# A two-layer graph network on one core: the planner of the instruction order gets a new table of TensorE's switches and tile durations, and new aims

## The chip, the cores and the metric

The kernel runs on one core of one Trainium2 chip, as one program. The time is the device time of one execution in microseconds (us). Five engines work side by side, each through a list of instructions of its own, in order: TensorE (PE in the profile; its weight loads are told apart as PEld), VectorE (DVE), ScalarE (ACT), GpSimd (POOL) and SyncE (SP, which only issues DMAs here). They wait for one another by semaphores.

## What is computed

Sixteen graphs (B = 16) of 1024 nodes with 256 features each, and an adjacency matrix of whole numbers for each. Two layers follow one another:

```python
# layer 0: attention of 8 heads of 32, masked by the graph, one linear map, residual
q, k, v = heads(x @ Wq), heads(x @ Wk), heads(x @ Wv)
e = einsum('whqd,whkd->whqk', q, k)
e = where(e >= 0, e, 0.2 * e)
attn = softmax(where(adj > 0, e, NEG), axis=-1)
h = layernorm(attn @ v)
x = layernorm(concat([h, x]) @ Wffn.T) + x
# layer 1: two graph attentions, layer norm, feed-forward of width 1024, layer norm
for W, a in ((W1, a1), (W2, a2)):
    Wh = h @ W                                  # h starts as x
    e = leaky_relu(Wh @ a[:256] + (Wh @ a[256:]).T, 0.2)
    h = softmax(where(adj > 0, e, NEG), axis=1) @ Wh
h = layernorm(x + h)
out = layernorm(h + relu(h @ w_ff1 + b_ff1) @ w_ff2 + b_ff2)
```

All of it is float32.

## The kernel before

For each batch (graph) `b` there are two kinds of work. The **attention of layer 0** is 8 heads of 8 tiles of 128 keys, 64 tiles for a batch. For each tile TensorE makes the scores of 128 keys by 1024 queries (line 612, two matmuls of 512 columns; the planner calls this kind `single`), ScalarE and VectorE make the leaky relu of them (lines 628 and 630), ScalarE the exponential (line 633), GpSimd multiplies by the mask of the graph (line 637), and the result `p` goes to the product with the values `v` (line 652). That product has only 32 output rows, so four matmuls, each for a quarter of the queries, lie side by side in TensorE's columns; the planner calls this kind `narrow`. The sums of the weights come from the same kind of product with a column block of minus ones. Two of these products a head are saved by adding tiles on VectorE first (line 682, `add_pair`): tiles 0 and 1, and tiles 2 and 3. So a head has 8 narrow products with `v` and 6 with minus ones. They are issued in groups of two tiles, four groups a head, 512 groups in all.

The **wide work** is all else on TensorE, the planner's kind `None`: projections of the next batch (lines 489 and 521), transposes (lines 369, 436, 702 and 846), the linear map of layer 0 (lines 778 and 781), both graph attentions (lines 901 and 926) and the feed-forward (lines 966 and 994). All of a batch after its attention is started by `rest(b)`, and runs while the attention of batch b+1 runs. The projections and the mask of batch b+1 are started by `project(b + 1, t0)` when the attention of batch b begins. Batch 0's attention therefore has nearly no wide work beside it, and the rest of batch 15 has no attention beside it.

The order in which every engine gets its instructions is planned in Python when the kernel is built. Each piece of work is a generator that yields its next operation with a cost in ns (`on(PE=880)`), waits for events, takes and gives buffers, and has an **aim**, the time at which it is due. `Order.run` keeps a clock for each engine, looks for the operations that could start within 300 ns of the earliest, takes the one with the smallest aim, emits its instructions, and moves the clock on by the cost. For TensorE it adds to the cost an entry of `SWITCH`, found by the kind of the operation before and the kind of this one; a pair that is not in the table costs nothing. A wrong cost changes no result and no instruction; it makes the plan believe that something is ready earlier or later than it is.

The aims come from two tables of shares of `SLOT` (253 us): `EARLY` for what belongs to the first batches, `AIM` for the others. `share(b, name)` chooses: `EARLY` for b below 2. For `project(b)` the choice is by b-1, so the projections and masks of batches 1 and 2 go by `EARLY`. `mask` and `mask_step` give the due times of the eight parts of the next mask after the start of the batch, `x` those of the input, `qk0`, `qk1`, `v0` and `v1` those of the projections; `rows`, `first0`, `graph0`, `second`, `normed` and so on those of the steps of `rest(b)`, and `ff` those of the feed-forward of its four pairs of row tiles. `pace(b)` says how fast the scores of a batch fall due; `fast0`, `fast1` and `fast15` stretch it for batches 0, 1 and 15. `lead` says how long before its due time a score tile may start.

Buffers that matter for the order: 6 tiles `p`, 2 score tiles in PSUM, 3 `misc` tiles in PSUM, 18 `pair` buffers, 2 masks, and one `job` for the feed-forward, so that there is one feed-forward at a time.

Of the kernel before, what the change touches and what calls it, by code (L numbers as in the profile page):

```python
# [34 lines left out]
class Order:  # L35
# [5 lines left out]
    HOP = dict(PE=53.0, ACT=35.0, DVE=36.0, POOL=80.0, SP=60.0)  # L41
    TAIL = dict(PE=163.0, ACT=103.0, DVE=84.0, POOL=42.0, SP=0.0)
    WINDOW = 300.0
    SWITCH = {(None, "narrow"): 93.0, ("single", "narrow"): 93.0, ("narrow", None): 93.0,
              ("narrow", "single"): 197.0, (None, "single"): 84.0}

    STRETCH = 3413.0
    WORK = 0.43
# [89 lines left out]
    def run(self):  # L138
        while self.active:
            could = []  # L140
            for th in self.active:
                costs, shared, delay, mode = th["op"]
                best = None
                for engine, cost in costs.items():
                    ready = th["ready"] + self.HOP[engine]
                    if th.get("last", ())[:2] == (engine, th["ready"]):
                        ready -= self.HOP[engine] + self.TAIL[engine]
                    t = asked = max(self.clock[engine], ready)
                    if shared and engine in ("DVE", "POOL"):
                        t = max(t, self.port[engine])  # L150
                    if best is None or t + cost < best[0] + best[2]:
                        best = t, engine, cost, asked
                could.append((best, th))
            first = min(c[0][0] for c in could)
            (t, engine, cost, asked), th = min((c for c in could if c[0][0] <= first + self.WINDOW),
                                        key=lambda c: (c[1]["aim"], c[1]["no"]))
            if th["op"][1] and engine in ("DVE", "POOL"):

                before = [c for c in could if c[1]["op"][1] and c[0][1] in ("DVE", "POOL")
                          and c[0][1] != engine and c[0][3] < asked]  # L160
                if before:
                    (t, engine, cost, asked), th = min(before, key=lambda c: (c[1]["aim"], c[1]["no"]))
            costs, shared, delay, mode = th["op"]
            self.active.remove(th)
            if engine == "PE":
                cost += self.SWITCH.get((self.mode, mode), 0.0)
                self.mode = mode
            end = self.clock[engine] = self.end(engine, t, cost)
            self.busy[engine] += cost
            if shared and engine in ("DVE", "POOL"):  # L170
                if engine == "DVE":
                    self.port["POOL"] = end - 54.0
                else:
                    self.port["DVE"] = end - 130.0
            self.now = t
            th["ready"] = end + self.TAIL[engine]
            th["last"] = engine, th["ready"]
            if delay:
                self.transfers = max(self.transfers, end + 1000) + 1450 * max(1, round(cost / 500))
                th["ready"] = max(end + delay, self.transfers + 1200)  # L180
                th["last"] = None, 0
            self.step(th, engine)
        stuck = {k: len(v) for k, v in list(self.waiting.items()) + list(self.queues.items()) if v}
        assert not stuck, f"threads that never end: {stuck}"


def on(shared=False, delay=0.0, mode=None, **costs):
    return "on", (costs, shared, delay, mode)
# [6 lines left out]
def wait(event):  # L195
    return "wait", event
# [37 lines left out]
def unshifted_path(  # L234
# [8 lines left out]
    nc = tc.nc  # L243
# [9 lines left out]
    G = 4  # L253
    GV = 2
    QN = N // 4
    ADDED = 2
    YW = D + 2
    NSUM = NT * H + 2 * NT
    NSCORE = 4 * NT
# [1 line left out]
    PACE = SLOT / (H * NT // 2)  # L261


    AIM = dict(mask0=0.7454, x=0.7836, x_step=0.0012, mask=0.7416, mask_step=0.0241, qk0=0.8169, qk1=0.7629,
               qk_step=0.0234, v0=0.8897, v1=0.9566, v_step=0.0513, rows=-0.1328, rows_step=0.039, first0=0.1101,
               first1=0.2264, graph0=-0.041, graph1=0.3629, graph_step=0.0128, second=0.3518, second_step=0.0609,
               normed=0.8572, normed_step=0.058, ff_wait=(None, 0, 1, 0), ff=(0.6792, -0.0021, 0.5781, 0.4984),
               ff_step=0.0549, fast0=0.4291, fast1=0.9756, fast15=0.6646, lead=1.5024)

    EARLY = dict(x=0.9697, x_step=0.0004, mask=0.7306, mask_step=0.0331, qk0=0.7893, qk1=0.9441, qk_step=0.026,  # L270
                 v0=0.8496, v1=0.9733, v_step=0.0532, rows=-0.1833, rows_step=-0.0236, first0=0.1365,
                 first1=-0.0311, graph0=-0.0903, graph1=-0.027, graph_step=0, second=0.3474, second_step=0.0327,
                 normed=0.781, normed_step=0.02, ff_wait=(None, 0, 1, 0), ff=(0.6698, 0.0209, 0.488, 0.4266),
                 ff_step=0.0422)

    const = ctx.enter_context(tc.tile_pool(name="const", bufs=1))
    sb = ctx.enter_context(tc.tile_pool(name="sb", bufs=1))
# [123 lines left out]
    def mask_part(b, t, halves):  # L401
# [29 lines left out]
        yield take("misc")  # L431
        pt = misc(BF)
        pairs = ab.bitcast(BF)
        yield on(PE=112 * n)
        for i in range(2 * n):
            nc.tensor.transpose(pt[:, i * P:(i + 1) * P], pairs[:, i * P:(i + 1) * P], ident_b)
        yield give("adjb")
# [20 lines left out]
    def x_pair(b, u):  # L458
        yield take("pair")
        xr = buf([P, 2, D], "pair", "xr")  # L460
        yield pause(1500)
        yield on(ACT=400, delay=3500)
        nc.scalar.dma_start(xr, x[b, u * 2 * P:(u + 1) * 2 * P, :].rearrange("(p i) d -> p i d", p=P))
        yield take("misc")
        pt = misc()
        yield on(PE=437)
        transposes(pt, [xr[:, i, :] for i in range(2)])
        yield give("pair")
        engine = yield evacuate(2 * D)
# [44 lines left out]
    def v_part(b, g, u):  # L514
        yield wait(("xT", b, u))
        yield take("misc")
        pa = misc()
        yield on(PE=880)
        for i in range(2):
            for dc in range(DC):  # L520
                nc.tensor.matmul(pa[:, i * P:(i + 1) * P], xTs[b][:, dc, (2 * u + i) * P:(2 * u + i + 1) * P],  # L521
# [69 lines left out]
    def all_scores():  # L591
        for b in range(B):
# [4 lines left out]
            for h in range(H):  # L597
                yield wait(("stack", b, h))
                q, kk = stacks[b, h]
                for t in range(NT):  # L600
# [5 lines left out]
                    else:  # L606
                        yield aim(t0, BIG)
                    ps = psum.tile([P, N], FT, tag="scores", name="ps_s")
                    yield on(PE=464, mode="single")
                    for nh in range(NH):  # L610
                        cols = slice(nh * HALF, (nh + 1) * HALF)
                        nc.tensor.matmul(ps[:, cols], kk[:, t * P:(t + 1) * P], q[:, cols], start=True, stop=True)  # L612
# [27 lines left out]
    def all_values():  # L640
        for b in range(B):
            for h in range(H):
# [9 lines left out]
                        nc.tensor.matmul(acc[i * DH:(i + 1) * DH, at:at + QN], w, p[:, i * QN:(i + 1) * QN],  # L652
                                         start=first, stop=last)

                added = []
                for d in range(0, NT, GV):
                    last, adds = d + GV == NT, d < ADDED * GV
                    for t in range(d, d + GV):
                        yield wait(("p", b, h, t))
                    if added:  # L660
                        yield wait(("p added", b, h, d - GV))
                    yield aim(begin[b] + (h * NT + d + 2) / 2 * pace(b), SLOT)
                    ps = [probs.pop((b, h, t)) for t in range(d, d + GV)]
                    for t, p in zip(range(d, d + GV), ps):
                        yield on(PE=430, mode="narrow")
                        product(v[:, t, c:c + DH], p, 0, t == 0, False)
                        yield aim(begin[b], BIG)
                    if adds:
                        yield start(add_pair(b, h, d, ps), begin[b] + (h * NT + d + 2) / 2 * pace(b))
                    for p in added if adds else added + ps:  # L670
                        yield on(PE=430, mode="narrow")
                        product(minus_ones, p, QN, False, last and p is ps[-1])
                        yield give("p")
                    added = ps[:1] if adds else []
                yield start(after_head(b, h, acc), begin[b] + (h + 1) * NT // 2 * pace(b))
                if h % G == G - 1:
                    yield give("v")
            yield start(rest(b), work.now)

    def add_pair(b, h, d, ps):  # L680
        yield on(DVE=1180, shared=True)
        nc.vector.tensor_tensor(ps[0], ps[0], ps[1], op=OP.add)  # L682
        yield give("p")
        yield fire(("p added", b, h, d))

    def after_head(b, h, acc):
        if h == 0:
# [9 lines left out]
        yield give("acc")  # L697
        yield take("misc")
        pt = misc()
        yield on(PE=437)  # L700
# [50 lines left out]
    def rows_pair(b, u):  # L751
# [12 lines left out]
        yield on(PE=437)  # L764
        transposes(pt, rows)
        yield fire(("hn used", b, u))
        yield take("pair")
# [20 lines left out]
        yield take("pair")  # L788
        yield take("misc")
        pt = misc()  # L790
        yield on(PE=437)
        transposes(pt, rows)
        yield give("pair")
        yield wait(("b2", b, u))
# [9 lines left out]
        for t in tiles:  # L804
            yield take("misc")
            pa = misc()
            yield on(PE=880)
# [28 lines left out]
    def first_half(b, s, nh):  # L836
# [4 lines left out]
            yield wait(("row", b, s, t))  # L841
        yield take("misc")
        pt = misc()
        yield on(PE=437)
# [70 lines left out]
    def normed_pair(b, u, big, y2):  # L915
# [6 lines left out]
        for i, t in enumerate(tiles):  # L922
            for half in range(2):
                yield on(PE=1728)
                for j in range(half * NT // 2, (half + 1) * NT // 2):
                    nc.tensor.matmul(pa[:, i * D:(i + 1) * D], big[:, j, t * P:(t + 1) * P], y2[:, j, :D],  # L926
                                     start=(j == 0), stop=False)
            yield on(PE=218)
            as_rows(pa, i, x1, i)
        yield fire(("weighed", b, u))  # L930
        yield give("pair")
# [4 lines left out]
        rT = buf([P, DC, 2 * P], "pair", "rT")  # L936
        yield take("misc")
        pt = misc()
        yield on(PE=437)
        transposes(pt, rows)  # L940
        yield give("pair")
        for dc in range(DC):
# [37 lines left out]
    def feed_forward(b, u, rT):  # L980
# [9 lines left out]
        for i in range(2):  # L990
            for half in range(2):
                yield on(PE=1728)
                for hc in range(half * HC // 2, (half + 1) * HC // 2):
                    nc.tensor.matmul(pa[:, i * D:(i + 1) * D], hid[hc // 2][:, hc % 2, i * P:(i + 1) * P], wf2[:, hc, :],  # L994
                                     start=(hc == 0), stop=False)
            yield on(PE=218)
            as_rows(pa, i, rT, i)
        for _ in range(HC // 2 + 1):
            yield give("pair")
# [471 lines left out]
```

## Time and profile before

| what | value |
|---|---|
| median of 3 runs | 4397.64 us (4397.36 to 4398.8) |
| the profiled execution's own time | 4397.53 us |
| span of its instructions | 4395.7 us |
| mean granted clock of TensorE | 0.99 |
| TensorE busy | 4246.0 us, 97% of the span |
| VectorE, ScalarE, GpSimd busy | 81%, 68%, 55% |
| DMA | 344.87 MB, 78 GB/s in the mean |

The busy time of TensorE counts a matmul from its start to its modelled end; consecutive matmuls overlap, so the busy share doesn't tell how dense the stream is. The distance from the start of one matmul to the start of the next does. The scores of a batch are 128 matmuls of line 612, which gives the stages: the first of batch 0 starts at 37.1 us, of batch 1 at 203.5, of batch 2 at 473.3, of batch 4 at 1004.1, of batch 15 at 3910.8; the last narrow product of batch 15 ends at 4173.4 us. From batch 4 to batch 15 a batch takes 264.2 us.

### The profile page before, as it was taken

How to read it: one execution, taken by the hardware profiler on the slowest of the kernel's cores; microseconds unless marked ns; L12 is line 12 of the kernel's file. 1: busy time of each engine (PE TensorE's matmuls, PEld its weight loads, DVE VectorE, ACT ScalarE, POOL GpSimd, SP SyncE). 2: the span in 40 equal slices, each digit the busy share in tenths (PEclk: the TensorE clock that was granted, in tenths of full speed). 3: DMA queues.
4: the chain of work that ended last, by engine and by line, in shares of the span. 5: the costliest groups of instructions: out<-in, count | busy, mean ns of one | idle time of the engine just before them, and what ended most of it. 6: DMA issues, size and time to landing. Idle time of an engine off the chain costs nothing.

```text
span 4395.7 us, 77297 instructions
## 1 busy us (share of the span) xinstructions
PE 4246.0 (97%) x30539; PEld 3077.3 (70%) x30539; DVE 3543.5 (81%) x5525; ACT 2979.7 (68%) x4456; POOL 2418.1 (55%) x1033
## 2 busy tenths in 40 slices
PE   7888999999999999999999999999999999999898
PEld 4455767767677776767767677776767767677687
DVE  6878878878787888889788787888878788887853
ACT  6756667766767767776676767767776676766632
POOL 5856555554656646565564755636565564755700
PEclk9999999999999999999999999999999999999999
DMA  6423223232232323222232232313222232221100
GB/s 186 122 68 87 71 70 85 65 100 68 85 84 73 94 61 92 80 85 77 66 101 70 85 82 68 101 61 89 82 82 80 66 101 70 83 74 49 34 20 21
DMA packets 156287, 344.87 MB, mean 78 GB/s; under 512 B 21750, under 2 KB 24332, under 8 KB 155916
## 3 DMA queue, kind: packets, MB, share of 16 engines
q1 hardware_dynamic: 112140, 260.13, 20.5%
q10 hardware_dynamic: 43776, 79.71, 6.5%
q8 instruction: 243, 3.98, 0.4%
q14 instruction: 128, 1.05, 0.1%
HBM read 239.09 MB, written 100.66 MB: 77 GB/s over the span
## 4 chain that ended last, share of the span: by engine, by line
PE 81%; DVE 14%; ACT 3%; issue 2%; POOL 0%; DMA 0%; ACTq 0%; SPq 0%; DVEq 0%; POOLq 0%
PE ps_a L652 16%; PE ps_m L901 10%; PE ps_s L612 9%; PE ps_m L926 9%; PE ps_m L994 8%; PE ps_m L966 8%; DVE p L630 4%; PE ps_m L489 4%; PE ps_m L810 3%; DVE att L863 3%; PE ps_m L778 3%; PE ps_m L781 2%; DVE att L866 2%; PE ps_m L369 2%; PE ps_m L521 2%
## 5 line engine op out<-in xcount | busy, mean ns | idle before, releaser
L637 POOL TENSOR_TENSOR p<-p,mask 128x1024 f32<-128x1024 f32 x1024 | 2417.3, 2377 | 1752.1 <-ACT p L633 1401.4
L630 DVE TENSOR_TENSOR p<-p,ps_s 128x1024 f32<-128x1024 f32 x1024 | 1221.2, 1215 | 356.0 <-ACT p L628 351.5
L633 ACT ACTIVATE p<-p 128x1024 f32<-128x1024 f32 x1024 | 1080.2, 1060 | 343.3 <-DVE p L630 319.0
L628 ACT ACTIVATE p<-ps_s 128x1024 f32<-128x1024 f32 x1008 | 989.9, 1022 | 285.8 <-PE ps_s L612 202.5
L612 PE MATMUL ps_s<-qs,ks 128*128 128x512 f32 x2048 | 639.1, 430 | 35.5 <-DVE p L630 35.3
L652 PE MATMUL ps_a<-p,v 128*32 128x256 f32 x8192 | 564.1, 388 | 13.2 <-POOL p L637 12.6
L612 PEld LDWEIGHTS ps_s<-qs,ks 128*128 128x128 f32 x2048 | 350.0, 190 | 213.5 <-issue 68.0
L926 PE MATMUL ps_m<-y,att 128*128 128x256 f32 x2048 | 487.0, 382 | 5.8 <-ACT y L871 5.8
L901 PE MATMUL ps_m<-y,att 128*128 128x258 f32 x2048 | 482.8, 383 | 3.1 <-ACT y L871 2.6
L966 PE MATMUL ps_m<-rT,wf 128*128 128x256 f32 x2048 | 472.7, 381 | 13.2 <-ACT z L327 7.3
L994 PE MATMUL ps_m<-wf,hid 128*128 128x256 f32 x2048 | 475.3, 380 | 7.4 <-DVE hn L709 7.2
L901 PEld LDWEIGHTS ps_m<-y,att 128*128 128x128 f32 x2048 | 385.2, 190 | 85.6 <-issue 12.9
L966 PEld LDWEIGHTS ps_m<-rT,wf 128*128 128x128 f32 x2048 | 380.6, 190 | 81.8 <-issue 11.0
L652 PE MATMUL ps_a<-p,minus_ones 128*32 128x256 f32 x6144 | 408.7, 384 | 25.2 <-DVE p L682 25.2
L994 PEld LDWEIGHTS ps_m<-wf,hid 128*128 128x128 f32 x2048 | 379.9, 190 | 72.9 <-PE ps_a L652 12.2
L926 PEld LDWEIGHTS ps_m<-y,att 128*128 128x128 f32 x2048 | 376.7, 190 | 64.6 <-issue 8.6
L652 PEld LDWEIGHTS ps_a<-p,v 128*32 128x32 f32 x8192 | 209.0, 109 | 286.3 <-issue 143.3
L682 DVE TENSOR_TENSOR p<-p 128x1024 f32<-128x1024 f32 x256 | 385.4, 1506 | 25.7 <-PE ps_a L652 25.6
L863 DVE SCALAR_TENSOR_TENSOR att<-first,second 128x1024 f32<-128x1024 f32 x256 | 393.7, 1538 | 4.5 <-ACT first L850 4.5
L866 DVE SCALAR_TENSOR_TENSOR att<-mask,att 128x1024 f32<-128x1024 fp8e4 x256 | 353.0, 1379 | 5.9
L652 PEld LDWEIGHTS ps_a<-p,minus_ones 128*32 128x32 f32 x6144 | 198.7, 111 | 166.9 <-DVE p L682 32.1
L871 ACT ACTIVATE y<-y,check 128x258 f32<-128x258 f32 x256 | 130.8, 511 | 254.7 <-DVE check L869 254.2
(105 smaller groups left out, 4373.3 us busy)
## 6 DMA issues: line engine op xcount, KB each, us to landing
qs<-qk_halves SPq DMA_DIRECT2D x256, 256.0 KB, 4.1
ks<-qk_halves SPq DMA_DIRECT2D x256, 256.0 KB, 5.1
adj_i<-in_adj_dram ACTq DMA_DIRECT2D x240, 256.0 KB, 3.1
qk_halves<-high SPq DMA_DIRECT2D x128, 256.0 KB, 3.6
qk_halves<-low SPq DMA_DIRECT2D x128, 256.0 KB, 2.7
xr<-in_x_dram ACTq DMA_DIRECT2D x64, 256.0 KB, 2.7
x_kept<-x SPq DMA_DIRECT2D x64, 256.0 KB, 2.0
x<-x_kept SPq DMA_DIRECT2D x64, 256.0 KB, 3.4
```

What stands on the lines that cost most here:

```text
L612: nc.tensor.matmul(ps[:, cols], kk[:, t * P:(t + 1) * P], q[:, cols], start=True, stop=True)
L628: nc.scalar.activation(p, ps, AF.Copy, scale=ALPHA)
L630: nc.vector.tensor_tensor(p, p, ps, op=OP.max)
L633: nc.scalar.activation(p, p, AF.Exp)
L637: nc.gpsimd.tensor_tensor(p, p, mask_of(b, t), op=OP.mult)
L652: nc.tensor.matmul(acc[i * DH:(i + 1) * DH, at:at + QN], w, p[:, i * QN:(i + 1) * QN], start=first, stop=last)
L863: nc.vector.scalar_tensor_tensor(e, first[:, 0, :], second[:, j:j + 1], first[:, 1, :], op0=OP.mult, op1=OP.max)
L866: nc.vector.scalar_tensor_tensor(e, mask_of(b, j), -1.0, e, op0=OP.mult, op1=OP.mult, accum_out=sums[:, j:j + 1])
L901: nc.tensor.matmul(pa[:, cols:cols + width], big[:, j, i * P:(i + 1) * P], rows[:, j, :width], start=(j == 0), stop=(j == NT - 1))
L926: nc.tensor.matmul(pa[:, i * D:(i + 1) * D], big[:, j, t * P:(t + 1) * P], y2[:, j, :D], start=(j == 0), stop=False)
L966: nc.tensor.matmul(pa[:, i * 2 * P:(i + 1) * 2 * P], wf1[:, dc, hc * P:(hc + 1) * P], rT[:, dc, :], start=(dc == 0), stop=(dc == DC - 1))
L994: nc.tensor.matmul(pa[:, i * D:(i + 1) * D], hid[hc // 2][:, hc % 2, i * P:(i + 1) * P], wf2[:, hc, :], start=(hc == 0), stop=False)
```

## The change

The table of switches, the costs of TensorE's tiles, and the two tables of aims are replaced. The code that adds tiles of `p` is written for any list of joins (`JOINS`, and `SUMMED`, which says after how many value products which tile is summed), with a second way of adding, by a DMA, that the list as it stands doesn't use.

```diff
-    SWITCH = {(None, "narrow"): 93.0, ("single", "narrow"): 93.0, ("narrow", None): 93.0,
-              ("narrow", "single"): 197.0, (None, "single"): 84.0}
+    SWITCH = {(None, "narrow"): 45.0, ("narrow", None): 250.0, ("narrow", "single"): 240.0}
...
             if delay:
-                self.transfers = max(self.transfers, end + 1000) + 1450 * max(1, round(cost / 500))
+                self.transfers = max(self.transfers, end + 1000) + (2700 if engine == "POOL" else
+                                                                    1450 * max(1, round(cost / 500)))
...
-    ADDED = 2
+    JOINS = (('dve', 0, 1), ('dve', 2, 3))
+    SUMMED = ((0, 4), (2, 6), (4, 6), (5, 6), (6, 8), (7, 8))
+    JOINCOST = 950
+    JOINDELAY = 3600
...
-    AIM = dict(mask0=0.7454, x=0.7836, x_step=0.0012, mask=0.7416, mask_step=0.0241, qk0=0.8169, qk1=0.7629,
-               qk_step=0.0234, v0=0.8897, v1=0.9566, v_step=0.0513, rows=-0.1328, rows_step=0.039, first0=0.1101,
-               first1=0.2264, graph0=-0.041, graph1=0.3629, graph_step=0.0128, second=0.3518, second_step=0.0609,
-               normed=0.8572, normed_step=0.058, ff_wait=(None, 0, 1, 0), ff=(0.6792, -0.0021, 0.5781, 0.4984),
-               ff_step=0.0549, fast0=0.4291, fast1=0.9756, fast15=0.6646, lead=1.5024)
-
-    EARLY = dict(x=0.9697, x_step=0.0004, mask=0.7306, mask_step=0.0331, qk0=0.7893, qk1=0.9441, qk_step=0.026,
-                 v0=0.8496, v1=0.9733, v_step=0.0532, rows=-0.1833, rows_step=-0.0236, first0=0.1365,
-                 first1=-0.0311, graph0=-0.0903, graph1=-0.027, graph_step=0, second=0.3474, second_step=0.0327,
-                 normed=0.781, normed_step=0.02, ff_wait=(None, 0, 1, 0), ff=(0.6698, 0.0209, 0.488, 0.4266),
-                 ff_step=0.0422)
+    AIM = dict(mask0=0.8371, x=0.5988, x_step=0.0268, mask=0.857, mask_step=0.0291, qk0=0.6738, qk1=0.9416,
+               qk_step=0.0361, v0=0.807, v1=0.3476, v_step=-0.0537, rows=-0.0018, rows_step=0.0173, first0=0.3845,
+               first1=-1.3281, graph0=-0.2862, graph1=0.1696, graph_step=0.0695, second=0.2637, second_step=0.042,
+               normed=0.9488, normed_step=0.0942, ff_wait=(None, 0, 1, 0), ff=(0.472, 0.0376, 2.3398, 0.5872),
+               ff_step=0.0391, fast0=-0.8204, fast1=0.7206, fast15=0.8254, lead=2.0198)
+
+    EARLY = dict(x=1.6274, x_step=-0.0013, mask=0.5124, mask_step=0.0274, qk0=0.7899, qk1=0.8273, qk_step=-0.0908,
+                 v0=0.373, v1=0.9683, v_step=0.0924, rows=-0.8129, rows_step=-0.0042, first0=0.0361,
+                 first1=-1.9834, graph0=-0.6468, graph1=-0.3393, graph_step=0.0724, second=0.2914,
+                 second_step=0.0258, normed=0.8933, normed_step=0.0734, ff_wait=(None, 0, 1, 0),
+                 ff=(1.7205, 0.3431, 1.0292, 0.5385), ff_step=0.0699)
...
-        yield on(PE=112 * n)
+        yield on(PE=30 + 140 * n)
...
-        yield on(PE=437)
+        yield on(PE=460)
...
-        yield on(PE=880)
+        yield on(PE=895)
...
-                    yield on(PE=464, mode="single")
+                    yield on(PE=466, mode="single")
...
-                added = []
+                ps = {}
+                begun = 0
                 for d in range(0, NT, GV):
-                    last, adds = d + GV == NT, d < ADDED * GV
+                    last = d + GV == NT
                     for t in range(d, d + GV):
                         yield wait(("p", b, h, t))
-                    if added:
-                        yield wait(("p added", b, h, d - GV))
-                    yield aim(begin[b] + (h * NT + d + 2) / 2 * pace(b), SLOT)
-                    ps = [probs.pop((b, h, t)) for t in range(d, d + GV)]
-                    for t, p in zip(range(d, d + GV), ps):
-                        yield on(PE=430, mode="narrow")
-                        product(v[:, t, c:c + DH], p, 0, t == 0, False)
+                    now = [t for t, at in SUMMED if at == d + GV]
+                    for t in now:
+                        for n in range(begun):
+                            if JOINS[n][1] == t:
+                                yield wait(("joined", b, h, n))
+                    due = begin[b] + (h * NT + d + 2) / 2 * pace(b)
+                    yield aim(due, SLOT)
+                    for t in range(d, d + GV):
+                        ps[t] = probs.pop((b, h, t))
+                        yield on(PE=434, mode="narrow")
+                        product(v[:, t, c:c + DH], ps[t], 0, t == 0, False)
                         yield aim(begin[b], BIG)
-                    if adds:
-                        yield start(add_pair(b, h, d, ps), begin[b] + (h * NT + d + 2) / 2 * pace(b))
-                    for p in added if adds else added + ps:
-                        yield on(PE=430, mode="narrow")
-                        product(minus_ones, p, QN, False, last and p is ps[-1])
+                    while begun < len(JOINS) and max(JOINS[begun][1:]) < d + GV:
+                        yield start(join(b, h, begun, ps), due)
+                        begun += 1
+                    for t in now:
+                        for n in range(begun):
+                            if JOINS[n][1] == t:
+                                yield wait(("joined", b, h, n))
+                        yield on(PE=434, mode="narrow")
+                        product(minus_ones, ps[t], QN, False, last and t == now[-1])
                         yield give("p")
-                    added = ps[:1] if adds else []
...
-    def add_pair(b, h, d, ps):
-        yield on(DVE=1180, shared=True)
-        nc.vector.tensor_tensor(ps[0], ps[0], ps[1], op=OP.add)
+    def join(b, h, n, ps):
+        how, to, by = JOINS[n]
+        for m in range(n):
+            if JOINS[m][1] in (to, by):
+                yield wait(("joined", b, h, m))
+        if how == "dve":
+            yield on(DVE=1180, shared=True)
+            nc.vector.tensor_tensor(ps[to], ps[to], ps[by], op=OP.add)
+        else:
+            yield on(POOL=JOINCOST, delay=JOINDELAY)
+            nc.gpsimd.dma_start(ps[to], ps[by], accum_op=OP.add)
         yield give("p")
-        yield fire(("p added", b, h, d))
+        yield fire(("joined", b, h, n))
...
-            yield on(PE=218)
+            yield on(PE=225)
```

More of the change, by code (lines that the diff above doesn't have):

```diff
@@ L699, in after_head @@
         pt = misc()
-        yield on(PE=437)
+        yield on(PE=460)
         for i in range(TPH):
@@ L763, in rows_pair @@
         pt = misc()
-        yield on(PE=437)
+        yield on(PE=460)
         transposes(pt, rows)
@@ L790, in rows_pair @@
         pt = misc()
-        yield on(PE=437)
+        yield on(PE=460)
         transposes(pt, rows)
@@ L806, in rows_pair @@
             pa = misc()
-            yield on(PE=880)
+            yield on(PE=895)
             w = YW + 2
@@ L843, in first_half @@
         pt = misc()
-        yield on(PE=437)
+        yield on(PE=460)
         for i in range(TPH):
@@ L938, in normed_pair @@
         pt = misc()
-        yield on(PE=437)
+        yield on(PE=460)
         transposes(pt, rows)
@@ L995, in feed_forward @@
                                      start=(hc == 0), stop=False)
-            yield on(PE=218)
+            yield on(PE=225)
             as_rows(pa, i, rT, i)
```

## The prediction

> **What bounds the kernel now.** I read the shares of the engines first, then the stages (cut at the first scores of batches 0, 1, 2, 4 and 15 and at the last narrow product), then who waited in them, then TensorE's own stream.
>
> ```profile
> PE 4246.0 (97%) x30539; PEld 3077.3 (70%) x30539; DVE 3543.5 (81%) x5525; ACT 2979.7 (68%) x4456; POOL 2418.1 (55%) x1033
> PE 81%; DVE 14%; ACT 3%; issue 2%; POOL 0%; DMA 0%; ACTq 0%; SPq 0%; DVEq 0%; POOLq 0%
> ```
>
> These are the busy times and the chain of waits. TensorE carries the program, and what can be won is the 149.7 us of the span in which it isn't busy (4395.7 - 4246.0), and what its switches cost. By stage (us; busy times of PE, PEld, DVE, ACT and POOL; granted clock):
>
> ```profile
> 0.00:37.00 37.00, 30.37 (x144) 19.41 (x144) 12.28 (x26) 15.42 (x35) 0.83 (x9) 1.00 0.87 284
> 37.00:203.40 166.40, 135.20 (x1163) 67.54 (x1163) 144.19 (x138) 128.20 (x150) 149.66 (x64) 0.93 0.50 137
> 203.40:473.20 269.80, 232.80 (x1724) 158.55 (x1720) 212.46 (x314) 174.55 (x245) 152.95 (x64) 0.92 0.27 77
> 473.20:1004.00 530.80, 515.05 (x3738) 371.73 (x3734) 433.35 (x672) 367.06 (x541) 300.62 (x129) 1.00 0.27 78
> 1004.00:3910.70 2906.70, 2874.85 (x20925) 2099.28 (x20922) 2414.74 (x3775) 2047.47 (x3054) 1653.73 (x705) 1.00 0.28 81
> 3910.70:4175.00 264.30, 249.17 (x1839) 179.44 (x1838) 222.97 (x338) 177.12 (x256) 160.32 (x65) 0.98 0.15 41
> 4175.00:4396.00 221.00, 208.55 (x1025) 181.31 (x1023) 103.50 (x264) 69.86 (x176) 0.00 (x0) 0.98 0.06 20
> ```
>
> The reader is to see where TensorE is idle (length less busy): 31.2 us in batch 0's attention, where GpSimd is the bound (149.7 of 166.4 us busy), 37.0 us in batch 1, 15.8 us in batches 2 and 3, 31.9 us in the eleven batches 4 to 14 (2.9 each), 15.1 us in batch 15, 12.5 us in the tail, 6.6 us before the first score. The waits of GpSimd between 190 and 260 us show a cause in batch 1; the waits of TensorE in batch 1, and then in batches 4 to 14, what the idle time consists of (total us, times, longest):
>
> ```profile
> POOL p L637 <- ACT mask L440: 38.2, 1, 38.2
> ...
> PE ps_a L652 <- DVE p L682: 17.5, 2, 9.5
> PE ps_m L926 <- ACT y L871: 5.8, 2, 5.4
> ...
> PE ps_m L369 <- DVE rT L386: 8.4, 10, 0.9
> PE ps_m L994 <- DVE hn L709: 7.2, 11, 0.7
> PE ps_m L966 <- ACT z L327: 7.1, 10, 0.7
> ```
>
> Batch 1's attention stands for 38.2 us because its mask is late. In the steady batches the waits are short and come once a batch, at the same places. Last, a stretch of TensorE's timeline (start, length, count):
>
> ```profile
> 898.25 0.61 PE L652 MATMUL ps_a<-p,minus_ones 128*32 128x256 f32 x8
> 898.80 1.20 PE L612 MATMUL ps_s<-qs,ks 128*128 128x512 f32 x4
> 899.84 3.65 PE L901 MATMUL ps_m<-y,att 128*128 128x258 f32 x16
> 903.42 1.07 PE L652 MATMUL ps_a<-p,v 128*32 128x256 f32 x16
> ```
>
> Eight narrow matmuls are two fours, 0.216 us from start to start; scores should start at 898.25 + 0.43 = 898.68 and start at 898.80. Four scores at 0.234 us should take 0.94 us and take 1.04. So leaving the narrow kind costs twice. Over all starts of the trace the medians of these excesses are 113 + 104 ns from narrow to scores, 114 + 104 ns from narrow to wide, 93 + 24 ns from wide or scores to narrow, and about 7 ns (-81 + 88) from wide to scores.
>
> **The change part by part.** No instruction is added or taken away: the joins are the same two on VectorE, the six sums come after the same groups with the same waits, and the DMA way isn't in the list. What moves is the order alone, so the sum is made of what TensorE's idle time and its switches can become.
>
> *Switches.* The trace has 547 runs of narrow products (511 entered from wide work, 36 from scores; 294 left to wide, 252 to scores), each entered and left once, at 117 + 218 = 335 ns: 183 us. Groups that stay whole need 512 runs, so 35 runs or 11.7 us could go; as many more would cost 11.7 us. The new table prices a trip wide-narrow-wide at 295 ns where the old one had 186, nearer to 335; wide-narrow-scores at 285 (290 before; 334 in the trace); scores to narrow at nothing, where the trace has 117. A wide-to-wide tile of transposes takes 436 ns in the trace, and the plan now believes 460 (437 before). So the table is truer for one trip of two and no truer otherwise, and I give it no gain of its own: **0**, between -11.7 and +11.7.
>
> The row here is the excess at both ends of a run; a matmul takes 380 ns and the next starts 216 ns after it, so that a full drain would add 164 ns, two of them 328. The Trainium skill (TensorEngine Tiling (Array Packing), Key Properties) says that a change of the tiling mode, unlike a change of tile, drains the engine; the trace's 335 agrees. That rule speaks against the table's cheap entries of 45 and 0 ns: entering all 547 runs from scores would by the table save 547 x 45 = 25 us and end at some 4348, by the rule nothing.
>
> *Start (batches 0 and 1).* The parts of the mask of batch 1 were due from 0.7306 to 0.7306 + 7 x 0.0331 = 0.962 of a slot of 253 us after batch 0's start, and are due from 0.512 to 0.704: the last one 65 us earlier. That is more than the 38.2 us that GpSimd waited, so its attention can go on where batch 0's ends. The input x of batch 1 falls due later (0.97 to 1.63 slots), which costs nothing as long as TensorE has gaps in batch 0, and it has 31.2 us of them. What can be won is bounded by the idle time of the stage, 37.0 us; 17.5 us of that are two waits for a join on VectorE, which the mask doesn't touch by itself. The other side: if the late x delays the scores instead, the same loss comes a second time, +37. Nearest to the rest of the row (37.0 - 17.5 = 19.5): I take **-15**.
>
> *Batches 2 to 14.* Batches 2 and 3 have 7.9 us idle each and the others 2.9; if all were like the others, 10 us would go, and if all were as the two are, 11 x 5.0 = 55 us would come. If every short wait went, 47.7 us would. The waits of the steady batches (0.7 us each) are of a size that one switch off by 0.1 to 0.2 us can make or end, and the plan has new errors beside old ones. I take **-5**, half of the ten.
>
> *Batch 15 and the tail.* Batch 15 idles 15.1 us against 2.9: there is too little wide work beside its attention. The feed-forward of the third pair of a batch now falls due 2.34 slots after it is ready (0.58 before), and the pace of batch 15 is slower (0.66 to 0.83), both of which keep wide work for it. The gain is 12 us at most; as much is lost if the kept work only lengthens the tail. I take **-5**.
>
> Sum: -15 - 5 - 5 = -25 us from the execution's own 4397.5 (span 4395.7 and 1.8 around it; the median is 0.1 us above): **4372 us**.
>
> **The rivals.** *A tighter plan throughout.* Steady batches lose 1.9 of their 2.9 us and, with 32 narrow runs a batch for 34.9 (384 in eleven batches), 2.9 x 0.335 = 1.0 us more: 2.9 x 13 = 38 us; with -20 at the start, 4340. For it: the same wait comes in ten of eleven batches, so one aim can remove it everywhere. Against: those 2.9 us are 1% of a batch already.
>
> *Attention starved by late inputs (the slower side).* The x of batch 2 also goes by the early table: due 1.63 x 253 = 412 us after batch 1's start, while batch 2's scores began 270 us after it. TensorE has only 37 us of gaps in batch 1, so work with smaller aims goes ahead of x, and then q, k, their way through DRAM and the scores come late. The rest of batch 1 is done meanwhile, but the attention that is left over runs at the end with too little wide work beside it: a tile takes GpSimd 2.377 us (its row in the page), and TensorE some 1.4 us (0.47 for scores, 14/8 narrow products of 0.43, and half a run's 0.335), so each such tile leaves 1.0 us idle. A delay of 412 - 270 = 142 us is, at 64 tiles in 264 us, 34 tiles; with a few of them covered some 31 us are lost: 4428. It decides from a delay of 37 us (9 tiles, 9 us). For it: the size of the move, and that buffers held by feed-forwards 2.34 slots late are missing elsewhere. Against: q and k themselves are due at 0.79, and nothing but x stands ahead of them.
>
> *Nothing that counts.* The aims reorder work that waits in the shadow of TensorE's stream, the table's errors trade places, gains at the start are given back by a mask or a join later: 4397, within 9 us. For it: TensorE was busy for 34.2 of the 38.2 us in which the mask was awaited.
>
> **How the numbers follow.** Chances: forecast (4372, from 4350 to 4388) 0.43; tighter plan 0.14; starved attention 0.28; nothing 0.15. About 0.2%, 9 us, is what a measurement of this kernel can tell from no change. Faster is the first two, 0.57; same 0.15; slower 0.28. The range goes down to 4325 (start -37, batches 2 to 14 -24, batch 15 -12), and up to 4430, past the starved case; about 0.18 is left outside.
>
> **What would show it.** Right: the wait of GpSimd for the mask around 205 us falls from 38.2 us to under 10, batch 2's scores start between 450 and 465 us (473.3 before), a steady batch stays between 263.5 and 264.5 us, batch 15 idles under 12 us, narrow runs stay between 512 and 570. Wrong: the distance between first scores of batches 1 and 2 grows above 280 us (starved), a steady batch falls under 262.5 (tighter), or it rises above 265.5, which no case here has: then the new prices, too low at the entry, set waits in every batch, and the time passes 4410.

## The result, and the profile after

| | before | after |
|---|---|---|
| median | 4398.22 us (4397.36 to 4399.35, 4 runs) | 4350.27 us (4348.61 to 4352.09, 4 runs) |
| ratio | | 0.9891, 95% interval 0.9874 to 0.9908 |
| span of the profiled execution | 4395.7 us | 4348.6 us |
| first scores of batches 1, 2, 4, 15 | 203.5, 473.3, 1004.1, 3910.8 us | 228.9, 484.3, 1003.5, 3871.7 us |
| from one batch to the next, batches 10 to 15 | 264.3 us | 260.0 us |
| from batch 15's first scores to the end | 484.9 us | 476.9 us |

The kernel is 47.9 us faster. Of the 47.1 us of the span, 0.6 lie before batch 4, 38.5 in batches 4 to 14 (2906.7 to 2868.2 us), 8.0 behind the first scores of batch 15. Batches 5 to 14 alone gave 45.1 (2644.6 to 2599.5 us); batch 4 took 6.6 us longer.

The busy times and the chain of waits of the changed kernel:

```profile
PE 4228.2 (97%) x30539; PEld 3088.8 (71%) x30539; DVE 3602.3 (83%) x5535; ACT 2997.0 (69%) x4446; POOL 2494.4 (57%) x1033
PE 87%; DVE 8%; ACT 2%; issue 1%; POOL 1%; ACTq 0%; POOLq 0%; DVEq 0%
```

The same number of matmuls and a chain that is TensorE's by 87% where it was 81%. The other counts show that the plan decides more than the order: for some copies out of PSUM it also takes the engine on which it believes them done first, and ScalarE has ten operations fewer and VectorE ten more (4456 to 4446, 5525 to 5535). A changed cost or aim can thus change an instruction too. The stages of the changed kernel, cut at the same events as before (us; busy times of PE, PEld, DVE, ACT, POOL; granted clock), and a stretch that holds only batches 5 to 14:

```profile
38.10:228.90 190.80, 148.70 (x1217) 72.48 (x1217) 144.68 (x148) 135.31 (x158) 142.20 (x63) 0.89 0.47 134
228.90:484.30 255.40, 221.72 (x1641) 149.48 (x1637) 201.57 (x297) 172.29 (x240) 152.81 (x65) 0.92 0.28 78
484.30:1003.50 519.20, 509.87 (x3729) 368.06 (x3725) 431.07 (x656) 371.47 (x552) 300.21 (x128) 1.00 0.27 78
1003.50:3871.70 2868.20, 2860.48 (x20957) 2114.95 (x20956) 2488.64 (x3814) 2056.73 (x3031) 1737.47 (x706) 1.00 0.29 82
3871.70:4130.50 258.80, 250.01 (x1860) 183.24 (x1858) 221.75 (x339) 179.72 (x267) 160.86 (x65) 0.99 0.16 44
...
1272.20:3871.70 2599.50, 2597.74 (x19044) 1921.28 (x19042) 2258.72 (x3471) 1867.82 (x2750) 1575.91 (x641) 1.00 0.29 82
```

In ten whole batches TensorE is idle for 1.8 us (2599.5 - 2597.74). The view of who waited for whom, for TensorE in that stretch, has no row at all; the kernel before has these in the ten batches from 1266.2 to 3910.8 us (total us, times, longest):

```profile
PE ps_m L369 <- DVE rT L386: 8.4, 10, 0.9
PE ps_m L966 <- ACT z L327: 7.1, 10, 0.7
PE ps_m L994 <- DVE hn L709: 6.5, 10, 0.7
PE ps_m L846 <- ACT first L850: 2.5, 10, 0.2
PE ps_m L436 <- DVE rT L386: 1.0, 6, 0.2
```

The same wait comes ten times in ten batches, because from batch 5 on the matmuls between two first scores stand in exactly the same sequence of lines in every batch, in both kernels. A batch takes 4.35 us less: 2.5 us of idle time (2.65 to 0.13 in gaps over 60 ns), 1.0 us for 32 narrow runs in place of 35 at 335 ns, and 0.8 us in smaller shifts within the stream.

The start is another matter. GpSimd's waits between 200 and 300 us:

```profile
POOL p L640 <- PE ps_m L865: 21.1, 1, 21.1
POOL p L640 <- ACT p L636: 15.3, 8, 6.2
POOL p L640 <- issue: 2.6, 2, 1.5
```

No wait for the mask of batch 1 is left (it was 38.2 us): its last part was copied at 213 us, 30 us earlier. But after head 0 of batch 1 GpSimd waits 21.1 us, while TensorE, busy all that time, runs mostly lines 797, 800 and 829 of the rest of batch 0 before the next scores. And batch 0's own attention takes 190.8 us where it took 166.4: GpSimd is busy for 142.2 of the 190.8 us where it was for 149.7 of the 166.4. One wait of 5.9 us is for the mask of batch 0, whose last part now comes at 57.5 us instead of 37.2; most of the others are for line 636 (the exponential), 24.4 us without the wait before the first tile where it was 10.4.

### The profile page after: what moved, and what is told of

It is laid out like the page before. It is cut to its first block, busy times and chain, and to the rows that moved or that the text cites. A ratio compares the mean times of both kernels' runs of the same rounds, so it can differ in the third digit from the quotient of the medians.

```text
span 4348.6 us, 77431 instructions
## 1 busy us (share of the span) xinstructions
PE 4228.2 (97%) x30539; PEld 3088.8 (71%) x30539; DVE 3602.3 (83%) x5535; ACT 2997.0 (69%) x4446; POOL 2494.4 (57%) x1033
## 4 chain that ended last, share of the span: by engine, by line
PE 87%; DVE 8%; ACT 2%; issue 1%; POOL 1%; ACTq 0%; POOLq 0%; DVEq 0%
PE ps_a L655 18%; PE ps_s L615 11%; PE ps_m L920 10%; PE ps_m L945 10%; PE ps_m L1013 9%; PE ps_m L985 9%; PE ps_m L492 4%; PE ps_m L829 3%; PE ps_m L797 2%; PE ps_m L800 2%; PE ps_m L372 2%; PE ps_m L524 2%; DVE p L633 2%; DVE att L885 1%; PE ps_m L721 1%
## 5 line engine op out<-in xcount | busy, mean ns | idle before, releaser
L640 POOL TENSOR_TENSOR p<-p,mask 128x1024 f32<-128x1024 f32 x1024 | 2493.5, 2454 | 1633.0 <-ACT p L636 1198.6
L655 PE MATMUL ps_a<-p,v 128*32 128x256 f32 x8192 | 561.2, 391 | 22.4 <-POOL p L640 21.1
L698 DVE TENSOR_TENSOR p<-p 128x1024 f32<-128x1024 f32 x256 | 400.6, 1565 | 14.2 <-PE ps_a L655 13.8
```

What stands on the lines that cost most here:

```text
L640: nc.gpsimd.tensor_tensor(p, p, mask_of(b, t), op=OP.mult)
L698: nc.vector.tensor_tensor(ps[to], ps[to], ps[by], op=OP.add)
```

## The experiments

Three theories stood at first: A, the new aims carry the gain; T, the truer costs carry it; C, aims and costs were fitted to one another.

**Each half alone, the start alone, and a cost moved by 2 ns.** The changed kernel with the old table of switches and the old tile costs:

```diff
-    SWITCH = {(None, "narrow"): 45.0, ("narrow", None): 250.0, ("narrow", "single"): 240.0}
+    SWITCH = {(None, "narrow"): 93.0, ("single", "narrow"): 93.0, ("narrow", None): 93.0, ("narrow", "single"): 197.0, (None, "single"): 84.0}
-        yield on(PE=460)
+        yield on(PE=437)
...
```

> The changed kernel with the old table of switches and the old costs of TensorE's tiles; the new aims stay. Theory A (the aims carry the gain: they take away the short waits that came once in each steady batch and cut 34.9 narrow runs a batch to 32): 4345 to 4365 us, steady batch 260.0 to 261. Theory T (the table carries it: the plan is better because its costs are truer): 4385 to 4400, steady batch 263.5 or more. Theory C (aims and table were fitted to one another, and either alone is worth little): 4365 to 4385, steady batch 261 to 263.5.

4575.15 us, ratio 1.0398 (1.038 to 1.0415). The mirror of it, new table and costs, with the whole of `AIM` and `EARLY` of the kernel before:

```diff
-    AIM = dict(mask0=0.8371, x=0.5988, ...
+    AIM = dict(mask0=0.7454, x=0.7836, ...
-    EARLY = dict(x=1.6274, x_step=-0.0013, ...
+    EARLY = dict(x=0.9697, x_step=0.0004, ...
```

> The changed kernel with the old aims; the new table and tile costs stay. Theory A: no gain, 4390 to 4410 us, steady batch 264 to 265.5. Theory T: most of the gain, 4350 to 4370, steady batch under 261.5. Theory C: worse than before, as the old aims were fitted to the old table: 4400 to 4430, steady batch 264.5 to 267.

4519.12 us, ratio 1.0275 (1.0257 to 1.0292). Only the start aimed as before:

```diff
-    AIM = dict(mask0=0.8371, ..., fast0=-0.8204, fast1=0.7206, ...)
+    AIM = dict(mask0=0.7454, ..., fast0=0.4291, fast1=0.9756, ...)
-    EARLY = dict(x=1.6274, x_step=-0.0013, ...
+    EARLY = dict(x=0.9697, x_step=0.0004, ...
```

> The changed kernel with the old early aims and the old mask0, fast0 and fast1: what belongs to batches 0 and 1 and to the preparation of batches 1 and 2 is aimed as before. The changed kernel reached batch 4 at 1003.5 us with 9 us less of TensorE's work done than the kernel before at 1004.1. If the start is separable from the rest: batch 1's scores at 203 to 210 us again, steady batch 260.0, total 4337 to 4347. If the new early aims are what the steady batches' pattern grows from: steady batch over 261 and total over 4360.

4496.13 us, ratio 1.0216 (1.0199 to 1.0233). And the control:

```diff
-                        yield on(PE=434, mode="narrow")
+                        yield on(PE=436, mode="narrow")
```

> The changed kernel with one cost of the plan moved by a hair: a narrow product costs 436 ns instead of 434. A control. Theories A and T: within 6 us of the changed kernel (4344 to 4356), steady batch 259.5 to 260.7. Theory C: the order falls apart into another one, 4360 to 4400, steady batch over 261.

4400.71 us, ratio 1.0001 (0.9991 to 1.001): 2 ns in the plan's cost of one kind of product, and the whole gain is gone. A and T fall. C fares little better: it had new aims on the old costs keep part of the gain, and they are far slower than before; it had old aims with new costs slower, but by some 30 us at most; only for the control it was near, 0.7 us above its range. For the start aimed as before the second expectation has the direction. What happens is seen from batch to batch (us from first scores to first scores, from batch 4 on):

```
before              262.1 264.3 264.3 264.4 265.6 264.3 264.3 264.3 264.3 264.3 264.3
after               268.7 259.9 260.0 259.9 259.9 260.0 260.0 260.0 260.0 259.9 260.0
new aims, old costs 286.4 264.2 276.6 274.7 272.2 284.5 279.8 277.5 272.0 274.4 278.7
old aims, new costs 274.8 266.2 286.1 264.7 269.5 288.1 266.2 270.5 286.9 273.9 273.3
start as before     274.0 268.1 274.2 271.2 278.5 259.0 274.6 279.2 275.7 270.5 271.3
436 for 434         265.1 271.1 271.8 266.9 260.0 260.0 260.0 260.0 260.0 260.0 260.0
```

Both good kernels fall into a sequence that repeats. The three that were made by halves never do. The control wanders through batch 7 and from batch 8 on repeats in the same 260.0, with the very sequence of 1904 matmuls a batch that the changed kernel has. Its two states by window, batch 5 and batch 9 (columns as above):

```profile
1287.80:1558.90 271.10, 262.54 (x1902) 190.99 (x1901) 221.19 (x344) 186.55 (x273) 152.54 (x64) 1.00 0.28 78
2357.60:2617.60 260.00, 259.82 (x1909) 192.19 (x1906) 225.94 (x348) 187.00 (x275) 157.73 (x65) 1.00 0.29 82
```

8.6 us idle in the one batch, 0.2 in the other, with a full clock in both. What TensorE waits for in the control from batch 4 to batch 8 (1022.8 to 2357.6 us), and then in the kernel with old aims and new costs (1013.7 to 4034 us):

```profile
PE ps_m L985 <- ACT hid L994: 8.5, 9, 1.3
PE ps_m L920 <- ACT hid L994: 1.7, 2, 0.9
...
PE ps_m L945 <- DVE hn L728: 49.1, 3, 16.4
PE ps_s L615 <- DVE p L633: 11.1, 10, 2.5
PE ps_m L985 <- ACT hid L994: 10.9, 11, 1.7
```

Most of it goes to `ps_m`: wide work that waits for what another engine still does, in the worst case 16.4 us behind line 728, the end of a head on VectorE.

**Is it the change, or any such order?** The kernel before with 431 for 430, and the changed kernel with another cost moved by 2 ns, whose matmuls stay in the repeating sequence:

```diff
-                        yield on(PE=430, mode="narrow")
+                        yield on(PE=431, mode="narrow")
```

> The kernel before with a narrow product at 431 ns instead of 430 in the plan. Theory C (each of the two orders is a lucky one: its batches fall into a pattern that repeats, and nearly any other cost breaks the pattern): 4460 to 4540 us, the distance between the first scores of batches wanders between 260 and 285. Rival R (only the new aims are so touchy; the old ones were sturdy): 4390 to 4410, 264 to 265 a batch.

```diff
-        yield on(PE=460)
+        yield on(PE=462)
```

> The changed kernel with four transposes at 462 ns instead of 460 in the plan; the order on TensorE differs in few places and stays in its pattern. Theory C: what counts is whether the pattern holds, not the cost: 4344 to 4357 us, steady batch 260.0. Rival R2 (a plan that is wrong by 2 ns is itself the harm): about 4400, as with the narrow products moved by 2 ns.

The first takes 4518.82 us, ratio 1.0272 (1.0255 to 1.0289), with 266 to 295 us a batch: the order before was as touchy, and R falls. The second takes 4349.91 us (ratio 0.9886, 0.987 to 0.9903), with 260.0 us a batch: R2 falls. A cost that is off by 2 ns does no harm by itself; the order that grows from it may. So the first four runs say that a fitted pair of costs and aims was taken apart; they don't say what either is worth. That needs aims fitted to each table.

**Each table with aims of its own.** In the next six kernels all of `AIM` and `EARLY` was varied at random, about half an hour for each (the last is the best of four such), until the plan fell into a repeating sequence. First the old costs, from the old aims, and the new ones, from the new aims:

> Old table and old tile costs with aims that were varied until the plan, by its own clock, ends a little earlier than the plan of the kernel before and falls into a repeating pattern. Theory T2 (within a pattern the table decides: with the old table the plan doesn't see that leaving the narrow kind costs 218 ns, so waits of 0.2 to 0.9 us stay in every batch on the chip): steady batch 264.0 to 266, 4375 to 4405 us, and waits of TensorE for rT, z, hn or their like once in each batch. Rival A2 (the table doesn't matter, a pattern is a pattern): steady batch under 262.5 without such waits, 4350 to 4370.

> New table and costs with the new aims varied in the same way, from the changed kernel on; the pattern of the steady batches stays, the start is another. Theory T2 and C: steady batch 260.0, total within 10 us of the changed kernel, 4340 to 4355. If the order of the start on the chip isn't what the plan thinks: 4355 to 4375.

The old table gives 4411.94 us, ratio 1.0024 (1.0014 to 1.0033), and 265.9 us a batch; its waits of TensorE from 1262.9 to 3921.9 us, ten batches:

```profile
PE ps_m L439 <- DVE hn L728: 11.8, 10, 1.2
PE ps_m L721 <- ACT mask L443: 5.4, 10, 0.5
PE ps_s L615 <- DVE p L633: 4.0, 10, 0.4
PE ps_m L721 <- DVE hid L991: 3.3, 10, 0.6
PE ps_m L372 <- DVE rT L389: 2.4, 10, 0.3
```

Another sequence than before, and again a handful of places where TensorE is a little early in every batch. T2 had this right, only the total is 7 us above its range. The new table with varied aims takes 4361.21 us (0.991, 0.9894 to 0.9927): 260.0 us a batch once more, with 5 us lost before batch 5 and 5 us after batch 15's first scores; the total is in its second expectation, and only half of it for the reason given there. It is hardly a second sequence: of the 1904 matmuls of a batch all but four (one tile of transposes) stand where the changed kernel has them.

Then the parts of the table apart. New switches with old tile costs (the second part of the first diff), old switches with new tile costs (its first part), and the medians of the trace as a table:

```diff
-    SWITCH = {(None, "narrow"): 45.0, ("narrow", None): 250.0, ("narrow", "single"): 240.0}
+    SWITCH = {(None, "narrow"): 117.0, ("single", "narrow"): 117.0, ("narrow", None): 218.0, ("narrow", "single"): 217.0, (None, "single"): 7.0}
```

> The new table of switches with the old costs of the tiles, and the new aims varied until the plan falls into a repeating pattern again. Theory S (it is the price of leaving the narrow kind, 240 to 250 ns, that keeps waits out of the pattern): steady batch 259.8 to 261, at most one named wait of TensorE in a steady batch, 4345 to 4375 us. Theory D (it is the longer tile durations, which put a margin of some 20 ns on every small tile): waits of TensorE stay in every batch, steady batch over 262.5, 4385 to 4410.

> The mirror of it: the old table of switches with the new costs of the tiles, aims varied in the same way. Theory S: waits of TensorE in every batch, steady batch 264 to 267, 4400 to 4435 us. Theory D: hardly a wait, steady batch 260 to 262, 4360 to 4385.

> Old costs of the tiles and a table with the medians of the trace: 117 ns into the narrow kind, 218 out of it to wide work, 217 to scores, 7 from wide to scores; aims varied in the same way. Theory S would have a plan with these prices hold on the chip: what waits TensorE has, the plan knew of; few different places (at most three in a steady batch), steady batch 262 to 264.5, as the search found only a looser pattern. Rival (the sums of the table, not its single entries, matter, and any margin will do): more than three waiting places a batch and over 264.5.

> The table with the medians of the trace (117 in, 218 and 217 out, 7 from wide to scores) together with the new, longer costs of the tiles; aims varied in the same way. Theory M (margin: it is not the single entry but a plan that is by 1 to 2 us a batch slower on TensorE than the chip, so that what TensorE needs is always there in time): named waits of TensorE under 1.5 us in a steady batch, steady batch 262 to 264, as the pattern found is a looser one, 4365 to 4395 us. Rival E (it is the form of the new table, a cheap entry and a dear exit): as with the same table and the old costs, waits of over 3 us a batch, 264.5 to 266, 4395 to 4415.

In the repeating batches (distance between first scores of batches 10 and 15, divided by five; in brackets TensorE's idle time a batch in gaps over 60 ns; then the median of the runs):

| table of switches | old tile costs | new, longer tile costs |
|---|---|---|
| old | 264.3 (2.65), 4398.22; searched again 265.9 (3.28), 4411.94 | 263.25 (1.73), 4396.41 |
| new | 262.85 (2.11), 4401.73 | 260.0 (0.13), 4350.27; searched again 260.0 (0.13), 4361.21 |
| medians of the trace | 265.0 (4.58), 4406.79 | 262.15 (1.54), 4369.20 |

The kernel before took 4397.95 to 4401.75 us in the median beside these kernels. The new switches alone (ratio 1.0005, 0.9995 to 1.0014) and the new tile costs alone (0.9991, 0.9982 to 1.0001) are level with it in the whole time. Their waits of TensorE from 1600 to 3900 us, the new switches alone first:

```profile
PE ps_m L372 <- DVE y L328: 12.0, 8, 1.5
PE ps_m L829 <- DVE x L817: 2.3, 8, 0.3
PE ps_m L945 <- ACT y L890: 2.2, 9, 0.3
...
PE ps_m L1013 <- ACT xT L330: 5.6, 9, 0.6
PE ps_m L439 <- DVE hn L728: 4.5, 8, 0.6
PE ps_m L439 <- DVE rT L389: 3.4, 8, 0.4
```

S falls as it stood: the new switches alone leave three waiting places a batch, and the truest prices of all, those of the trace, with the old durations do worst, with six places against S's own limit of three. D had the new switches alone right in all it said, and falls by its mirror, which has three places as well and a batch of 263.25 us where D had 262 at most. E falls: the trace's prices with long durations wait 1.54 us a batch, not over 3, and that kernel is faster than the one before, ratio 0.993 (0.9913 to 0.9947). M's expectation for it came in full: named waits of 1.4 us a batch ((5.9 + 2.9 + 2.7) / 8), 262.15 us, 4369.20. For the trace's prices with old and with long durations the waits of TensorE from 1600 to 3900 and from 1800 to 3900 us:

```profile
PE ps_m L985 <- ACT hid L994: 21.2, 27, 1.0
PE ps_s L615 <- DVE p L633: 6.2, 9, 0.7
PE ps_m L372 <- DVE y L366: 4.8, 8, 0.6
...
PE ps_s L615 <- DVE p L633: 5.9, 8, 0.8
PE ps_m L492 <- ACT hid L994: 2.9, 8, 0.4
PE ps_m L985 <- DVE hT L389: 2.7, 8, 0.3
```

The one division that holds over all eight kernels is by the tile costs, and for the idle time alone: 2.1 to 4.6 us a batch with the old ones, 0.1 to 1.7 with the new ones. It doesn't hold for the batch itself: the new switches with old costs take 262.85 us, the old switches with new costs 263.25. The old costs are the steps of the trace or a little less (437 for four transposes that take 4 x 109 = 436, but 430 for two fours that take 432, and 880 for eight products of line 521 that take 8 x 112 = 896); the new ones are longer by 2.3 us a batch in all (28 tiles of transposes by 23 ns, 16 of projections by 15, 8 mask tiles by 86, and smaller ones), and most of them are longer than the trace has them. A plan that believes TensorE a little slower than it is may have what TensorE needs ready in time; that fits, but no run shows it apart from the aims that came with it. M's sum over the whole table is not the measure, though: new switches with old costs come short of the chip's switches (295 for 335 ns a trip) and wait less than the trace's medians with the same old costs, which don't.

What stays open: apart from the kernels before and after, each entry comes from searches of half an hour (four of them for the last), and the depth of the search behind the changed kernel's aims isn't known. So how much of its 260.0 is owed to a table that lets a good sequence hold, and how much to a better sequence found, can't be told apart: there are two sequences for the old table and one for each of the others. Why the trace's prices with old durations wait the most wasn't tried further. None of these kernels beats the changed one; with 460 replaced by 462 it is level with it.

## Why the prediction was right, and where it wasn't

The time lay on the side forecast, at nearly twice the forecast gain (47.9 for 25), and 0.3 us above the lower bound given with the forecast (4350). That it lay there at all is luck in good part: by the sum's own stages the start lost 11.0 us where 15 were to come, batches 2 to 14 gave 50.1 where 5 were, and the two errors partly cancelled. The direction was right for a reason that the text had named but priced low.

- *What bounds.* Right. Idle time and switches of TensorE gave 3.5 of the 4.35 us that a repeating batch got shorter. That the order alone moves was not quite so: ten operations, on balance, went from ScalarE to VectorE.
- *Switches, 0.* The number fell from 547 runs to 532, within the bounds (5 us), and in a steady batch from 35 to 32 (1.0 us). A change costs what it did: 113 + 104, 114 + 104 and 93 + 24 ns are again the medians. (Of the 547 runs before, 295 left to wide work, not 294.) Narrow runs entered from scores, which the new table makes free, rose from 36 to 55, 35 of them in batch 0, and their entry costs 91 + 24 ns in the median, so nothing was saved there, as the Trainium skill has it (TensorEngine Tiling (Array Packing), Key Properties: a change of mode drains the engine); the trace agrees.
- *Start, -15.* Wrong: batches 0 and 1 took 11.0 us more (batch 2's first scores at 484.3 instead of 473.3 us). The mask did come earlier and GpSimd's wait for it went, but 21.1 us of another wait came in its place, and batch 0's attention ended at 233.4 us instead of 212.3. TensorE's idle time rose from 31.2 to 42.1 us in batch 0 and fell from 37.0 only to 33.7 in batch 1. The step took a wait on GpSimd for a loss, though TensorE was busy for 34.2 of those 38.2 us, which the text itself held against it further down.
- *Batches 2 to 14, -5.* This is the term that was mis-sized: it measured -50.1, of which 11.6 in batches 2 and 3 and 38.5 in batches 4 to 14. The bounds nearly had it (47.7 us if every short wait went, and every one went in batches 5 to 14), but the middle was taken as if the waits were scattered. They recur at the same places because the order repeats, so one good sequence removes them in ten batches at once. The rival of the tighter plan said just this, at 2.9 us a batch where 4.35 came, and with 20 us at the start that didn't come; it had 0.14.
- *Batch 15 and the tail, -5.* About right: 8.0 us, with 8.8 us idle in batch 15 (258.80 - 250.01) against 15.1.
- *The table, no gain of its own.* The argument, that the table is not truer entry by entry, was sound. That it therefore does nothing doesn't follow: the kernels with the new tile costs idle less in a repeating batch, whichever table of switches they have. What the table is worth in time stays open, as each half of it, with aims of its own, left the whole time where it was.
- *The starved attention* didn't come: the x of batch 2 was late (from 290 us on, against 255 to 270), and batch 2 still followed batch 1 by 255.4 us. Its shape came in the kernels made by halves, by other waits.
- *What would show it.* The mask's wait, the idle time of batch 15 and the number of runs came as said; batch 2's scores at 484.3 us (450 to 465 forecast) and the steady batch of 260.0 (263.5 to 264.5) did not, and by the text's own marks pointed to the tighter plan.

## What to carry to other kernels

In an order that is planned for a loop of like stages, look whether the order repeats, and read the one repeating stage: half a microsecond there was worth 5 us over ten batches. Don't judge a cost or an aim of such a plan by changing it alone: 2 ns in one cost lost the whole gain of 48 us here, and 1 ns in the kernel before made it some 120 us slower. Fit the rest to it again, and compare the stage beside the total. Durations planned slightly too long for the engine that bounds went with less idle time in these eight kernels; that is worth a try elsewhere, and not yet a rule.

## What was not expected of the hardware

How exactly the chip repeats itself: batches with the same order, or with one tile moved, take 259.9 to 260.0 us each, seven to ten of them on end, in four kernels (the changed one, the two made from it with a cost moved by 2 ns, once they repeat, and the one with the new table and varied aims), with all engines and some 80 GB/s of transfers at work. It isn't without exception: in the kernel before, nine of ten batches with the same order take 264.3 to 264.4 us and one 265.6. In the five kernels that wander, no batch from batch 4 on has the order of the one before it as long as they do.
